# Layer 2's opening: one pipeline over both samples, and a first block whose spectra are formed four rows at a time

## The chip, the cores and the metric

The kernel runs on one core of one Trainium2 chip. The metric is device time in microseconds (us) of that core for one execution of the whole program; several executions are timed and their median is the time of the kernel. A separate profiled execution gives the page and the trace.

## What is computed

Two images of 128 channels by 64 by 64 points, held in the core's memory as X, pass four layers; each adds its output to X after a group normalisation. Layers 0 and 3 are attention over all 4096 points, layer 1 is a set of convolutions. Layer 2, the one concerned here, multiplies quaternion-valued images in the Fourier domain:

```python
xs = jnp.stack([x[:, :q], x[:, q:2 * q], x[:, 2 * q:3 * q], x[:, 3 * q:]])
Xs = jnp.fft.rfft2(xs, s=(GRID_H, GRID_W), axes=(-2, -1))
Ws = jnp.stack([kr_w + 1j * ki_w, kr_x + 1j * ki_x, kr_y + 1j * ki_y, kr_z + 1j * ki_z])
C = jnp.einsum('piohw,qbihw->pqbohw', Ws, Xs)
Pw = C[0, 0] - C[1, 1] - C[2, 2] - C[3, 3]
Px = C[0, 1] + C[1, 0] + C[2, 3] - C[3, 2]
...
o = jnp.fft.irfft2(P, s=(GRID_H, GRID_W), axes=(-2, -1))
```

Every frequency (64 by 33 of them) has its own 128 by 128 real-valued mixing of the channels, so the weights are far larger than the images.

## The kernel before

Layer 2 is the function `_layer2`. All its compute instructions keep the order in which the program text issues them, engine by engine (`_in_order`); an engine that waits holds everything queued behind it. What that order is follows from Python generators: a generator does a piece of work at each step, and `alongside(main, side, steps)` issues `steps` pieces of the side work evenly between the pieces of the main work, and the rest after it.

**Transforms over h** (lines 849 to 895 of the kernel before). For each sample b in turn, the 64 image columns are cut into eight groups of eight. `normalized` (ScalarE, line 860) scales and shifts a group into a tile g; `columns` (TensorE, line 870, and VectorE, line 876) transposes it four times into PSUM and copies it out as gt; `transformed` (TensorE, line 883, and ScalarE, line 884) multiplies by a constant matrix in four matmuls and copies the result into y. A skewed loop issues, in iteration i, `normalized(i)`, `columns(i - 1)` and `transformed(i - 2)`. The loop runs to its end for sample 0 before it begins for sample 1. The statistics of sample 1 (mean and inverse deviation, tile st) are worked out by VectorE, TensorE and GpSimd between the groups of sample 0; from them comes the small tile shift (line 852), which `normalized` reads.

**Blocks of frequencies** (line 897 on). The 32 rows of spectra in y are taken in eight blocks of four. Each block serves two products: one with the rows themselves ("direct", weights of four frequency rows), one with their mirror images. For a row, `transposed` (TensorE line 912, ScalarE line 918) brings y's row into yt, its inner `transformed` (TensorE, line 925) does the transform over w into the PSUM bank pe, and `placed` writes 12 signed copies of it into the tile e (ScalarE, line 948, for the even rows of a pair; VectorE, line 950, for the odd ones). `rows_in` does these for a pair of rows; `copies` does the last of them alone.

`products` (TensorE, line 1008) is 17 steps, one for each pair of frequencies j; a step is four matmuls, one for each row s of the block, each of which writes its own group of 32 output partitions. Each matmul shows as two records in the trace. After j = 3, 7, 11 and 15, and after the last, VectorE transposes the PSUM bank in blocks into z (line 1017), and two VectorE operations form pz (line 1025). The four banks of PSUM are called z0, z4, z8 and z12, two more are tagged bank, two pe.

In the first block the direct rows of both pairs go in ahead of anything else, pair by pair; the mirrored rows are then formed again, transposes and transforms included, beside the first product. The weights of a product (2112 KB twice, line 823) come by DMA from the SP queue into one of two buffers; the load for a product is issued when the product before the last has released its buffer.

Of the kernel before, what the change touches and what calls it, by code (L numbers as in the profile page):

```python
# [10 lines left out]
F32 = mybir.dt.float32  # L11
# [7 lines left out]
CH = 512  # L19
# [783 lines left out]
def _layer2(ctx, tc, X, weights, cst, src, here=None, there=None, beside=None):  # L803
# [26 lines left out]
    with tc.tile_pool(name="l2_a", reuse_waits="tile", bufs=3) as ap, tc.tile_pool(  # L830
        name="l2_aps", reuse_waits="tile", bufs=4, space=PSUM
    ) as aps:
        def stats(b, st):
            return _stats_steps(
                nc,
                ap,
                lambda: aps.tile([128, CH], F32, tag="pt", name="ps_stat"),
                X[:, b, :],
                cst,
                mhalf,  # L840
                st,
            )

        st = here
        if st is None:
            st = ap.tile([128, 2], F32, tag="st", name="st")
            for _ in stats(0, st):
                pass
        for b in range(B):
            xw = X[:, b, :].rearrange("p (h w) -> p w h", w=W)  # L850
            shift = ap.tile([128, 1], F32, tag="shift", name="shift")
            nc.vector.scalar_tensor_tensor(shift, st[:, 0:1], -1.0, st[:, 1:2], ALU.mult, ALU.mult)
            scale = st[:, 1:2]
            if b + 1 < B:
                st = ap.tile([128, 2], F32, tag="st", name="st")
                steps = stats(b + 1, st)

            def normalized(i):
                g = ap.tile([128, 8, H], F32, name="g")
                nc.scalar.activation(  # L860
                    g, xw[:, 8 * i : 8 * i + 8, :], AF.Identity, bias=shift, scale=scale
                )
                for _ in range(2):
                    next(steps, None)
                return g

            def columns(i, g):
                pt = aps.tile([128, CH], F32, tag="pt", name="ps_pt")
                for n in range(4):
                    nc.tensor.transpose(  # L870
                        pt[:, n * 128 : (n + 1) * 128],
                        g[:, 2 * n : 2 * n + 2, :].rearrange("p w h -> p (w h)"),
                        ident,
                    )
                gt = ap.tile([128, CH], F32, name="gt")
                nc.vector.tensor_copy(gt, pt)
                return gt

            def transformed(i, gt):
                py = aps.tile([128, CH], F32, tag="py", name="ps_py")  # L880
                for n in range(4):
                    cols = slice(n * 128, (n + 1) * 128)
                    nc.tensor.matmul(py[:, cols], gt[:, cols], k["fwd_h"], start=True, stop=True)
                nc.scalar.copy(
                    y[:, b, 8 * i : 8 * i + 8, :, :].rearrange("p w c f -> p (w c f)"), py
                )

            gs, gts = {}, {}
            for i in range(W // 8 + 2):
                if i < W // 8:  # L890
                    gs[i] = normalized(i)
                if 1 <= i <= W // 8:
                    gts[i - 1] = columns(i - 1, gs.pop(i - 1))
                if i >= 2:
                    transformed(i - 2, gts.pop(i - 2))

    two = ctx.enter_context(tc.tile_pool(name="l2_two", reuse_waits="tile", bufs=2))
    with tc.tile_pool(name="l2_e", reuse_waits="tile", bufs=4) as ep, tc.tile_pool(
# [21 lines left out]

        def transformed(m, yt):

            pe = bank("pe")
            for b in range(B):
# [64 lines left out]

        def products(ws, e, pz):  # L990

            z = two.tile([128, PAIRS, 2, 4, 16], F32, name="z", bufs=1)
            zf = z.rearrange("p j n a x -> p (j n a x)")
            for j in range(PAIRS):
                last = j == PAIRS - 1
                if j % 4 == 0:
                    ph = bank() if last else pzp.tile([128, CH], F32, tag=f"z{j}", name="ps_z")  # L1000
                for s in range(4):
                    fw = s * FW + 2 * j
# [11 lines left out]
                    )  # L1014
                if j % 4 == 3 or last:
                    lo, n = j // 4 * CH, (j % 4 + 1) * 128
                    nc.vector.transpose(zf[:, lo : lo + n], ph[:, :n])
# [56 lines left out]

        def alongside(main, side, steps):

            done = 0
            for n, _ in enumerate(main):
                while done < steps * (n + 1) / PAIRS:
                    next(side, None)  # L1080
                    done += 1
            for _ in side:
                pass
# [4 lines left out]
        es = [None, None]  # L1088
        first = spectra(0)
        for i in (0, 2):  # L1090
            for _ in rows_in(0, first[i : i + 2], (0,), es):
                pass
        before, later = None, []
        for kb in range(BLOCKS2):
# [10 lines left out]
            else:  # L1105
                later = side
                side, n = [rows_in(0, first[i : i + 2], (1,), e) for i in (0, 2)], 10
            alongside(products(rows_of_weights(kb, False), e[0], pzs[0]), chain(*side), n)
            side, n = [turned(pzs[0], direct)], 4
# [1488 lines left out]
```

## Time and profile before

| what | us |
|---|---|
| median of 3 timed executions | 4012.31 (4012.15 to 4015.99) |
| profiled execution, its own time | 4012.48 |
| its span in the profile | 4010.7 |
| PE / DVE / ACT busy in the span | 3857.8 / 3197.1 / 3247.0 |
| layer 2, first normalisation to last y of the transforms over h | 1795.55 to 1829.78 |
| first block's first product, first and last record | 1837.01 to 1854.39 |
| first block's second product, first record | 1858.84 |

Times within the program are counted from the start of the span. A row of the trace gives the start, the duration, the engine (PE is TensorE, PEld its weight loads, DVE VectorE, ACT ScalarE, POOL GpSimd, SP the queue that issues DMAs), the source line, the operation, what it writes and reads, shapes, and how many records are merged; in brackets stands how long the engine had been idle before it and what released it.

### The profile page before, as it was taken

The numbers are of one execution on the slowest core, as the hardware profiler recorded it, in microseconds if no ns is written. First come the engines' busy times: TensorE is split into PE (matmuls) and PEld (weight loads), VectorE is DVE, ScalarE is ACT, GpSimd is POOL, SyncE is SP. The second block draws the span as 40 slices with busy tenths as digits, with TensorE's granted clock in tenths as the row PEclk, the third lists the DMA queues.
The fourth block names the chain that finished last, engine by engine and source line by source line (L and its number), as shares of the span: only waits on it lengthen the run. The fifth ranks groups of instructions, "written<-read, shape, count | busy, mean of one in ns | idle before, by whom it ended". The sixth has DMA issues, their size and how long they took to land.

```text
span 4010.7 us, 82168 instructions
## 1 busy us (share of the span) xinstructions
PE 3857.8 (96%) x35214; PEld 1318.5 (33%) x35214; DVE 3197.1 (80%) x3572; ACT 3247.0 (81%) x3955; POOL 86.2 (2%) x145
## 2 busy tenths in 40 slices
PE   7999999989999998997998999999999999999998
PEld 4511222353111124445664332232223222322222
DVE  6599999858999998995758777777777777776666
ACT  4499999736899983226645999999999999999998
POOL 1000000000000001000000000000000000000000
PEclk9999999999999999998999999999999999999999
DMA  1199960000000000004654100110002000110000
GB/s 51 24 201 189 187 98 2 1 2 2 2 2 2 2 1 13 6 38 176 268 215 149 33 31 26 53 46 30 27 25 74 30 27 25 43 48 6 6 6 4
DMA packets 193128, 217.59 MB, mean 54 GB/s; under 512 B 30441, under 2 KB 154345, under 8 KB 188658
## 3 DMA queue, kind: packets, MB, share of 16 engines
q1 hardware_dynamic: 192754, 212.25, 20.4%
q8 instruction: 278, 4.55, 0.5%
q14 instruction: 96, 0.79, 0.1%
HBM read 178.64 MB, written 98.57 MB: 69 GB/s over the span
## 4 chain that ended last, share of the span: by engine, by line
PE 81%; DVE 7%; issue 4%; ACT 3%; POOL 0%; DMA 0%; SPq 0%; POOLq 0%; ACTq 0%; DVEq 0%
PE ps_acc L2313 25%; PE ps_s L2290 19%; PE ps L1858 11%; PE ps L1866 11%; PE ps_bank L710 2%; PE ps_z L1008 2%; DVE sums L1889 2%; PE ps L1619 2%; DVE e L950 1%; PE ps_t L640 1%; PE ps_bank L590 1%; PE ps_bank L1062 1%; PE ps_bank L681 1%; PE ps_acc L2171 1%; PE ps_acc L2217 1%
## 5 line engine op out<-in xcount | busy, mean ns | idle before, releaser
L2304 ACT ACTIVATE weights<-ps_s 128x1024 f32<-128x1024 f32 x1920 | 1781.4, 1063 | 76.4 <-PE ps_s L2290 76.2
L2313 PE MATMUL ps_acc<-weights,vt 128*32 128x512 f32 x8192 | 1092.9, 605 | 0.0
L1889 DVE TENSOR_TENSOR sums<-sums,weights 128x2048 f32<-128x2048 f32 x384 | 854.2, 2283 | 3.5 <-ACT weights L1941 1.2
L2290 PE MATMUL ps_s<-q,k 64*128 64x512 f32 x4096 | 830.6, 469 | 4.3 <-DMA k<-stack 2.8
L1941 ACT ACTIVATE weights<-ps 128x1536 f32<-128x1536 f32 x512 | 740.6, 1446 | 6.9 <-PE ps L1866 6.9
L2290 PEld LDWEIGHTS ps_s<-q,k 64*128 64x128 f32 x4096 | 348.4, 184 | 936.6 <-ACT weights L2304 809.4
L1866 PE MATMUL ps<-q,k 32*64 32x512 f32 x8192 | 574.0, 612 | 3.6 <-ACT weights L1938 3.0
L1858 PE MATMUL ps<-weights,vt 128*32 128x512 f32 x4096 | 544.6, 604 | 0.0
L2262 DVE SCALAR_TENSOR_TENSOR exp_z<-exp_z,exp_m 128x1024 f32<-128x1024 f32 x384 | 468.9, 1221 | 9.3
L1938 ACT ACTIVATE weights<-ps 128x512 f32<-128x512 f32 x512 | 306.8, 599 | 75.4 <-PE ps L1866 36.5
L2246 DVE TENSOR_SCALAR exp_i<-ps_s 128x1024 int32<-128x1024 f32 x128 | 156.7, 1224 | 216.4 <-PE ps_s L2290 216.2
L2313 PEld LDWEIGHTS ps_acc<-weights,vt 128*32 128x32 f32 x8192 | 161.9, 108 | 309.3 <-issue 308.5
L1866 PEld LDWEIGHTS ps<-q,k 32*64 32x64 f32 x8192 | 120.0, 129 | 432.1 <-ACT weights L1938 381.6
L1858 PEld LDWEIGHTS ps<-weights,vt 128*32 128x32 f32 x4096 | 84.3, 108 | 390.9 <-issue 378.5
L662 DVE SCALAR_TENSOR_TENSOR X<-g,w,X 128x2048 f32<-128x2048 f32 x84 | 197.4, 2351 | 2.6
L2266 DVE SCALAR_TENSOR_TENSOR weights<-exp_z,exp_i 128x1024 f32<-128x1024 f32 x128 | 156.8, 1225 | 15.9 <-ACT weights L2304 0.5
L1889 DVE TENSOR_TENSOR sums<-weights 128x2048 f32<-128x2048 f32 x64 | 145.7, 2288 | 28.7 <-ACT weights L1941 27.9
L1619 PE MATMUL ps<-pad,diag 32*32 32x512 f32 x4032 | 151.8, 614 | 8.7 <-DVE qk L1630 4.1
L2262 DVE SCALAR_TENSOR_TENSOR exp_z<-exp_m 128x1024 f32<-128x1024 f32 x128 | 155.9, 1218 | 0.0
L1008 PE MATMUL ps_z<-w_ri,e 128*32 128x128 f32 x2048 | 137.5, 409 | 14.6 <-DVE e L950 12.4
L1619 PEld LDWEIGHTS ps<-pad,diag 32*32 32x32 f32 x4032 | 86.2, 104 | 69.2 <-issue 21.1
L950 DVE TENSOR_SCALAR e<-ps_pe 32x136 f32<-32x136 f32 (+1 forms) x352 | 104.4, 297 | 5.0
(314 smaller groups left out, 2953.5 us busy)
## 6 DMA issues: line engine op xcount, KB each, us to landing
w_ri<-w_r SPq DMA_DIRECT2D x16, 2112.0 KB, 7.9
w_ri<-w_i SPq DMA_DIRECT2D x16, 2112.0 KB, 13.7
stack<-qs SPq DMA_DIRECT2D x64, 256.0 KB, 2.1
q<-stack SPq DMA_DIRECT2D x128, 128.0 KB, 2.5
k<-stack SPq DMA_DIRECT2D x128, 128.0 KB, 2.5
stack<-ks SPq DMA_DIRECT2D x32, 256.0 KB, 2.1
w_r<-in_L_conv_kr_w SPq DMA_DIRECT2D x15, 528.0 KB, 12.3
w_r<-in_L_conv_kr_x SPq DMA_DIRECT2D x15, 528.0 KB, 12.5
```

The costliest lines, as they stand in the source:

```text
L662: nc.vector.scalar_tensor_tensor(xi, g[:, i : i + H // 2, j : j + W], w8[:, s : s + 1], xi, ALU.mult, ALU.add)
L1008: nc.tensor.matmul(out.rearrange("p (n f o) -> p n f o", n=2, f=2), e[:, s, 2 * j : 2 * j + 2, :].rearrange("p f x -> p (f x)"), w.rearran ...
L1619: nc.tensor.matmul(ps[r // 2][to, r % 2, :].rearrange("p (h w) -> p h w", w=W), diag[rows, grp, t, :], pad[rows, y0 : y0 + ROWS, t % 3 : t ...
L1858: nc.tensor.matmul(out[rows, :], lhs(rows), w[:, j, :], start=first, stop=stop)
L1866: nc.tensor.matmul(bank[64 * h : 64 * h + 64, :], k1[rows, kt * 128 + 64 * h : kt * 128 + 64 * h + 64], q1[rows, qb * CH : (qb + 1) * CH], ...
L1889: nc.vector.tensor_add(parts[p].rearrange("p j c -> p (j c)"), t.rearrange("p j c -> p (j c)"), w.rearrange("p j c -> p (j c)"),)
L1938: nc.scalar.activation(held[n][:, 0, :], single, AF.Exp)
L1941: nc.scalar.activation(held[n][:, 1:, :], three, AF.Exp)
L2262: nc.vector.scalar_tensor_tensor(z, x, n, m, ALU.add, ALU.mult)
L2290: nc.tensor.matmul(ps[j // 2][:, j % 2, :], g.k[kt // 4][rows, j // 2, keys], g.q[qb][rows, j // 2, :], start=True, stop=True,)
L2304: nc.scalar.activation(w[0], ps[p], AF.Exp)
L2313: nc.tensor.matmul(g.ac[32 * j : 32 * j + 32, :], g.vt[:, kt, j // 2, i : i + 2, :].rearrange("p a d -> p (a d)"), w[:, i, :], start=(at = ...
```

## The change

The loop over samples around the transforms over h becomes one loop over 16 groups, n = 0 to 15, with the same skew of two; the sample is n // 8. The statistics of sample 1 are finished, and its shift formed, ahead of group 8. The copies into y of groups 7, 9, 11, 13 and 15 are issued on VectorE instead of ScalarE.

In the first block all four rows are transposed first and then transformed, rows 3 and 4 into the product banks z8 and z12, since there are only two pe banks. Their direct copies follow without a gap. The mirrored copies of rows 1 and 2 are read from the same pe banks; only rows 3 and 4 are formed again for their mirror. The first block's direct product runs by pairs of rows: rows 1 and 2 for the first 16 frequency pairs, then rows 3 and 4 for the same 16, then the last frequency pair with all four rows, 33 steps in all. Eight pieces of side work are spread over these steps.

```diff
@@ -846,53 +846,65 @@
             st = ap.tile([128, 2], F32, tag="st", name="st")
             for _ in stats(0, st):
                 pass
-        for b in range(B):
-            xw = X[:, b, :].rearrange("p (h w) -> p w h", w=W)
+        def shifted(st):
             shift = ap.tile([128, 1], F32, tag="shift", name="shift")
             nc.vector.scalar_tensor_tensor(shift, st[:, 0:1], -1.0, st[:, 1:2], ALU.mult, ALU.mult)
-            scale = st[:, 1:2]
-            if b + 1 < B:
-                st = ap.tile([128, 2], F32, tag="st", name="st")
-                steps = stats(b + 1, st)
-
-            def normalized(i):
-                g = ap.tile([128, 8, H], F32, name="g")
-                nc.scalar.activation(
-                    g, xw[:, 8 * i : 8 * i + 8, :], AF.Identity, bias=shift, scale=scale
+            return shift
+
+        scales = [st]
+        shifts = [shifted(st)]
+        if B > 1:
+            scales.append(ap.tile([128, 2], F32, tag="st", name="st"))
+            steps = stats(1, scales[1])
+
+        def normalized(n):
+            b, i = divmod(n, W // 8)
+            if i == 0 and b > 0:
+                for _ in steps:
+                    pass
+                shifts.append(shifted(scales[b]))
+            xw = X[:, b, :].rearrange("p (h w) -> p w h", w=W)
+            g = ap.tile([128, 8, H], F32, name="g")
+            nc.scalar.activation(
+                g,
+                xw[:, 8 * i : 8 * i + 8, :],
+                AF.Identity,
+                bias=shifts[b],
+                scale=scales[b][:, 1:2],
+            )
+            for _ in range(2):
+                next(steps, None)
+            return g
+
+        def columns(n, g):
+            pt = aps.tile([128, CH], F32, tag="pt", name="ps_pt")
+            for k4 in range(4):
+                nc.tensor.transpose(
+                    pt[:, k4 * 128 : (k4 + 1) * 128],
+                    g[:, 2 * k4 : 2 * k4 + 2, :].rearrange("p w h -> p (w h)"),
+                    ident,
                 )
-                for _ in range(2):
-                    next(steps, None)
-                return g
-
-            def columns(i, g):
-                pt = aps.tile([128, CH], F32, tag="pt", name="ps_pt")
-                for n in range(4):
-                    nc.tensor.transpose(
-                        pt[:, n * 128 : (n + 1) * 128],
-                        g[:, 2 * n : 2 * n + 2, :].rearrange("p w h -> p (w h)"),
-                        ident,
-                    )
-                gt = ap.tile([128, CH], F32, name="gt")
-                nc.vector.tensor_copy(gt, pt)
-                return gt
-
-            def transformed(i, gt):
-                py = aps.tile([128, CH], F32, tag="py", name="ps_py")
-                for n in range(4):
-                    cols = slice(n * 128, (n + 1) * 128)
-                    nc.tensor.matmul(py[:, cols], gt[:, cols], k["fwd_h"], start=True, stop=True)
-                nc.scalar.copy(
-                    y[:, b, 8 * i : 8 * i + 8, :, :].rearrange("p w c f -> p (w c f)"), py
-                )
-
-            gs, gts = {}, {}
-            for i in range(W // 8 + 2):
-                if i < W // 8:
-                    gs[i] = normalized(i)
-                if 1 <= i <= W // 8:
-                    gts[i - 1] = columns(i - 1, gs.pop(i - 1))
-                if i >= 2:
-                    transformed(i - 2, gts.pop(i - 2))
+            gt = ap.tile([128, CH], F32, name="gt")
+            nc.vector.tensor_copy(gt, pt)
+            return gt
+
+        def transformed(n, gt):
+            b, i = divmod(n, W // 8)
+            py = aps.tile([128, CH], F32, tag="py", name="ps_py")
+            for k4 in range(4):
+                cols = slice(k4 * 128, (k4 + 1) * 128)
+                nc.tensor.matmul(py[:, cols], gt[:, cols], k["fwd_h"], start=True, stop=True)
+            copy = nc.vector.tensor_copy if n > 5 and n % 2 else nc.scalar.copy
+            copy(y[:, b, 8 * i : 8 * i + 8, :, :].rearrange("p w c f -> p (w c f)"), py)
+
+        gs, gts, every = {}, {}, B * (W // 8)
+        for n in range(every + 2):
+            if n < every:
+                gs[n] = normalized(n)
+            if 1 <= n <= every:
+                gts[n - 1] = columns(n - 1, gs.pop(n - 1))
+            if n >= 2:
+                transformed(n - 2, gts.pop(n - 2))
 
     two = ctx.enter_context(tc.tile_pool(name="l2_two", reuse_waits="tile", bufs=2))
     with tc.tile_pool(name="l2_e", reuse_waits="tile", bufs=4) as ep, tc.tile_pool(
@@ -918,9 +930,9 @@
             nc.scalar.copy(yt.rearrange("p b i -> p (b i)"), pt[:, : B * 128])
             return yt
 
-        def transformed(m, yt):
-
-            pe = bank("pe")
+        def transformed(m, yt, pe=None):
+
+            pe = bank("pe") if pe is None else pe
             for b in range(B):
                 nc.tensor.matmul(
                     pe[:, b * 8 * PAIRS : (b + 1) * 8 * PAIRS],
@@ -987,18 +999,22 @@
                     )
                 )
 
-        def products(ws, e, pz):
-
-
-
+        def products(ws, e, pz, by_rows=False):
 
             z = two.tile([128, PAIRS, 2, 4, 16], F32, name="z", bufs=1)
             zf = z.rearrange("p j n a x -> p (j n a x)")
-            for j in range(PAIRS):
+            whole = [(j, range(4)) for j in range(PAIRS)]
+            if by_rows:
+                whole = [(j, s) for s in ((0, 1), (2, 3)) for j in range(PAIRS - 1)] + whole[-1:]
+            phs = {}
+            for j, rows in whole:
                 last = j == PAIRS - 1
-                if j % 4 == 0:
-                    ph = bank() if last else pzp.tile([128, CH], F32, tag=f"z{j}", name="ps_z")
-                for s in range(4):
+                if j % 4 == 0 and rows[0] == 0:
+                    phs[j // 4] = (
+                        bank() if last else pzp.tile([128, CH], F32, tag=f"z{j}", name="ps_z")
+                    )
+                ph = phs[j // 4]
+                for s in rows:
                     fw = s * FW + 2 * j
                     if last:
                         w = ws[:, :, :, fw : fw + 1].to_broadcast([128, 2, 32, 2])
@@ -1012,7 +1028,7 @@
                         start=True,
                         stop=True,
                     )
-                if j % 4 == 3 or last:
+                if (j % 4 == 3 or last) and rows[-1] == 3:
                     lo, n = j // 4 * CH, (j % 4 + 1) * 128
                     nc.vector.transpose(zf[:, lo : lo + n], ph[:, :n])
                 yield
@@ -1072,11 +1088,11 @@
             for g in gens:
                 yield from g
 
-        def alongside(main, side, steps):
+        def alongside(main, side, steps, over=PAIRS):
 
             done = 0
             for n, _ in enumerate(main):
-                while done < steps * (n + 1) / PAIRS:
+                while done < steps * (n + 1) / over:
                     next(side, None)
                     done += 1
             for _ in side:
@@ -1087,8 +1103,13 @@
         ]
         es = [None, None]
         first = spectra(0)
+        yts = [transposed(m) for m in first]
+        places = [None, None] + [
+            pzp.tile([128, CH], F32, tag=f"z{n}", name="ps_z") for n in (8, 12)
+        ]
+        gots = [transformed(m, yt, pe) for m, yt, pe in zip(first, yts, places)]
         for i in (0, 2):
-            for _ in rows_in(0, first[i : i + 2], (0,), es):
+            for _ in copies(0, first[i : i + 2], gots[i : i + 2], (0,), es):
                 pass
         before, later = None, []
         for kb in range(BLOCKS2):
@@ -1104,8 +1125,13 @@
                 n += 6
             else:
                 later = side
-                side, n = [rows_in(0, first[i : i + 2], (1,), e) for i in (0, 2)], 10
-            alongside(products(rows_of_weights(kb, False), e[0], pzs[0]), chain(*side), n)
+                side, n = [copies(0, first[:2], gots[:2], (1,), e), rows_in(0, first[2:], (1,), e)], 8
+            alongside(
+                products(rows_of_weights(kb, False), e[0], pzs[0], kb == 0),
+                chain(*side),
+                n,
+                PAIRS if kb else 2 * PAIRS - 1,
+            )
             side, n = [turned(pzs[0], direct)], 4
             if nxt:
                 side = later + [rows_in(kb + 1, nxt[2:], (1, 0), es)] + side
```

The engines' instruction lists of the changed program differ from those before only in these places: in the order of the transforms over h from group 6 on, and in the first block up to its second product; from there on they are the same, instruction by instruction. Four transposes, four matmuls of the transform over w and two copies into yt fall away.

## The prediction

> **What bounds the kernel now.** I read the page first, for the whole, and then the trace of layer 2's opening alone, because the diff touches nothing else.
>
> ```profile
> span 4010.7 us, 82168 instructions
> PE 81%; DVE 7%; issue 4%; ACT 3%; POOL 0%; DMA 0%; SPq 0%; POOLq 0%; ACTq 0%; DVEq 0%
> ```
>
> TensorE carries 81% of the chain that ended last, nearly all of it in the attention layers, which stay as they are. So the prize is not a share of 4010.7 us; it is what can be cut from the stretch between the first normalisation of layer 2 (1795.55) and the moment from which both programs issue the same instructions in the same order. That moment is the start of the first block's second product, on the mirrored rows: 1858.84. The stretch is 63.3 us. The busy time of its four stages (columns: us, then PE, PEld, DVE, ACT, POOL busy, clock, DMA):
>
> ```profile
> 1795.50:1812.70 17.20, 14.30 (x100) 12.94 (x100) 11.07 (x23) 13.84 (x17) 0.55 (x1) 0.90 1.00 409
> 1812.70:1829.80 17.10, 13.89 (x97) 12.62 (x97) 5.54 (x8) 13.87 (x17) 0.00 (x0) 0.90 0.23 96
> 1829.80:1841.00 11.20, 5.15 (x30) 3.61 (x31) 7.23 (x24) 8.15 (x28) 0.00 (x0) 0.78 0.01 1
> 1841.00:1858.80 17.80, 13.39 (x154) 8.74 (x154) 11.21 (x31) 8.34 (x28) 0.00 (x0) 0.79 0.19 65
> ```
>
> No engine is full in any of them: these are latency-bound stages, so I followed the order of ScalarE, VectorE and TensorE in time. ScalarE at the change of sample:
>
> ```profile
> 1807.75 0.59 ACT L884 COPY y<-ps_py 128x512 f32<-128x512 f32 x1
> 1808.23 1.28 ACT L860 ACTIVATE g<-X,shift,st 128x512 f32<-128x512 f32 x1
> 1809.48 0.59 ACT L884 COPY y<-ps_py 128x512 f32<-128x512 f32 x1
> 1811.16 0.59 ACT L884 COPY y<-ps_py 128x512 f32<-128x512 f32 x1 [1.09 <-PE ps_py L883]
> 1812.20 0.59 ACT L884 COPY y<-ps_py 128x512 f32<-128x512 f32 x1 [0.46 <-PE ps_py L883]
> 1812.69 2.40 ACT L860 ACTIVATE g<-X,shift,st 128x512 f32<-128x512 f32 x2
> ```
>
> Three copies in a row, two of them waiting: the pipeline drains before sample 1 starts. VectorE in the first block:
>
> ```profile
> 1831.90 0.36 DVE L950 TENSOR_SCALAR e<-ps_pe,signs 128x136 f32<-128x136 f32 x1 [3.96 <-PE ps_pe L925]
> 1837.12 0.36 DVE L950 TENSOR_SCALAR e<-ps_pe,signs 128x136 f32<-128x136 f32 x1 [1.45 <-PE ps_pe L925]
> 1846.45 0.72 DVE L1017 STREAM_TRANSPOSE z<-ps_z 128x512 f32<-128x512 f32 x1 [5.57 <-PE ps_z L1008]
> 1853.98 0.72 DVE L1017 STREAM_TRANSPOSE z<-ps_z 128x512 f32<-128x512 f32 x1 [0.64 <-PE ps_z L1008]
> 1857.56 1.23 DVE L950 TENSOR_SCALAR e<-ps_pe 32x136 f32<-32x136 f32 x4
> ```
>
> VectorE stands 1.45 + 5.57 + 0.64 us here, and its last copies of e (the last line) release the second product. TensorE's products, by how many row groups (32 output partitions each) run side by side:
>
> ```profile
> 1837.01 0.65 PE L1008 MATMUL ps_z<-w_ri,e 128*32 128x128 f32 x4
> 1839.82 0.64 PE L1008 MATMUL ps_z<-w_ri,e 128*32 128x128 f32 x2 [2.16 <-ACT e L948]
> 1842.55 0.67 PE L1008 MATMUL ps_z<-w_ri,e 128*32 128x128 f32 x8
> 1858.84 0.66 PE L1008 MATMUL ps_z<-w_ri,e 128*32 128x128 f32 x8 [4.45 <-DVE e L950]
> 1878.82 0.64 PE L1008 MATMUL ps_z<-w_ri,e 128*32 128x128 f32 x6
> 1914.58 0.62 PE L1008 MATMUL ps_z<-w_ri,e 128*32 128x128 f32 x2 [0.88 <-DVE e L950]
> ```
>
> One matmul shows as two records. One group (x2), two (x4), three (x6) and four (x8) all take 0.62 to 0.67 us: groups beside each other are free, and fewer groups save nothing. This decides the forecast.
>
> **What the Trainium skill says.** "TensorE: Matmul & The Clock Gate", section "Measured speedup vs the span model", prices a pack of column tiles at one matmul's duration plus about 4 ns per further tile; the lines above agree (0.64 for one group, 0.67 for four). The same page, "Architectural detail: the array is 16× 32×32, not 1× 128×128", has ScalarE and VectorE as strict FIFO, so a waiting transpose holds the copies behind it; the trace agrees (e copies of 1847.09 stand behind the transpose of 1846.45). Its section "What's actually happening" has the array at half clock after an idle window of about 3.4 us; the trace agrees: four transposes of y take 1.12 us at 1841.51 and 0.71 at 1849.57. "TensorEngine Tiling (Array Packing)", "PSUM Bottleneck", advises both engines for emptying PSUM, which the change does for y; the trace of before has only ScalarE there.
>
> **Part 1: one pipeline over both samples.** Nothing is removed; from the seventh group of columns every odd y copy goes to VectorE (0.69 us, from the gt row of the same shape, against 0.59). Old: g7 starts 1808.23, the copy of y5 1809.48; then the drain, and g8 at 1812.69. New: g8 follows y5 after 0.48 (as 1807.75 to 1808.23), at 1809.96. Its shift now stands behind the seventh gt (end 1809.28) plus 0.15, 1809.43: in time, and the statistics' last step has been done since 1805.34 (1804.79 plus 0.55 on POOL).
>
> Does the rest run faster with ScalarE relieved? Old steady pace: about 1.70 us per group (1806.56, 1808.23; 1821.81, 1823.57, 1825.22). New, per pair: y copy 0.48, g 1.28, 0.05 to the transposes, 0.49 until the py matmuls, 1.06 for these, 0.04 to the next even y copy: 3.40 us. That is 1.70 per group again: the loop through TensorE's queue binds, not ScalarE (which would need 0.48 + 2 × 1.19 = 2.86). So this gives no pace, only the drain. Following it: y6 1811.16, y8 1814.56, y10 1817.96, y12 1821.36, g15 1821.84; the old tail from g15 to the last y is 1829.78 - 1825.22 = 4.56, so y ends at 1826.4. **Gain 3.4 us.** The moved copies ride in VectorE's idle time (5.54 busy of 17.10); without that cover they would cost 5 × 0.69.
>
> **Part 2: four rows of spectra at once, products by pairs.** Times from y's end (old 1829.78 = 0). Old: e of rows 1 and 2 from 1.66 (ScalarE) and 2.12 (VectorE), the second pair from 6.43 and 7.34, done at 11.1; first product's end about 24.6; second product's start 29.06.
>
> New. Four yt copies (0.33 each) instead of two, so e starts about 0.5 later: 2.17 and 2.65. No gap between pairs: ScalarE 2 × 3.55, to 9.3; VectorE 2 × 3.77, to 10.2. The first pair's mirrored copies follow at once, without new transforms (4 transposes, 4 matmuls and 2 yt copies fall away): to 12.9 and 14.0.
>
> TensorE can start rows 0 and 1 at 6.5. But a step (two passes, 0.46: at 1845.26, 32 records, four steps, take 2.05 us; less one record's 0.41, plus the 0.23 between passes, over four, is 0.46 to 0.47) costs the same with two groups as with four. The 17 four-group steps of 7.8 us become 16 + 16 + 1 = 33 steps, 15.2 us. In order: 16 steps, 6.5 to 13.9 (bank z8 free at 9.3, z12 at 10.2, before steps 9 and 13 need them); one step, 14.3; four transposes, 14.9; four steps, 16.7; the last two rows' transforms 1.12, 17.9; then twelve steps.
>
> VectorE's queue from 14.0: first z transpose when step j=3 is done, 16.5; the second stands behind steps j=5 to 7, which stand behind the transforms: 19.5. The mirrored copies of the fourth row are queued behind both. From 19.5 it hardly waits: 0.72, four copies 1.25, z 0.72, four copies 1.23, z 0.72, bank 0.32, the two pz operations 1.15, four copies 1.23, gaps 0.2: 27.0. So the second product starts at about 27.0 instead of 29.06. **Gain 2.1 us** (bounds 1.2 to 3: step 0.48 to 0.43).
>
> **Behind it** all shifts together. Weights: the third load is issued at the first product's end, 23.4, that is 3.6 us ahead of the second product instead of 4.4; old it was issued at 1854.44 and landed by about 1868 for a first use at 1878.82, and no product ever waits for a DMA, so 0.8 us costs nothing. SP's and POOL's instructions keep their order.
>
> Sum: 3.4 + 2.1 = 5.5 us. The profiled execution took 4012.48, so 4007.0; from the median shown, 4012.31, that is **4006.8**.
>
> **Rivals.** (a) Pairs are cheap: if two groups need half a step (0.23), rows 0 and 1 wait only for the banks, z4 is ready at about 15.7 and the second product starts at 23.1: part 2 gives 6.0, in all 9.4, 4002.9. For it: the one two-group line (x4) shows two passes of one matmul, not a run of different ones. Against: one, three and four groups agree, at both clocks (0.62 and 0.64 at full, 0.64 and 0.67 at half).
> (b) Little but the drain is won: TensorE stays at half clock through the thinner products, and the mirrored rows' transposes and transforms cost 1.12 + 2.18 (as at 1841.51 and 1843.15) instead of 0.6 + 1.12. That is 1.6 us before z4, so part 2 keeps 0.5: 3.9 in all, 4008.4; uncounted gaps could take another 2.
> (c) ScalarE's relief does raise the pace, to 2.86 per pair: 0.54 × 4 = 2.2 more, 4004.6. Against: the 3.40 loop.
> (d) Slower: half clock doubles a pair's step s. Once s is over about 0.49, TensorE sets every z transpose, and by the order above the second product starts at 12.1 + 32 s. At 0.92 that is 41.5, a loss of 12.4; less 3.4, 4021.3. Slower than before from s = 0.63 on. Against: passes at half clock kept the same 0.64 to 0.67.
>
> **How the numbers follow.** Forecast 0.62 (own range 4005 to 4008.5), (a) 0.18, (b) 0.11, (c) 0.05, (d) 0.04. A measurement of this kernel tells about 0.2%, 8.0 us, from no change; the forecast lies inside it, (a) outside. Faster 0.24 ((a), and (c) with some of the forecast's far end), same 0.71, slower 0.05. Range 4001.5 to 4010.8: (a) to most of (b).
>
> **What would show it.** Right: no run of three y copies; g8 about 0.5 after y5; y ends near 1826.4; pace still 3.4 per pair with ScalarE waiting for ps_py; pair products of 32 matmuls spread over about 7.4 us; VectorE idle before the first two z transposes; second product near 1853.4. A pair run of about 4 us would mean (a); pairs of g closer than 3.4, (c). Wrong altogether if the interval from second product to the end changes by more than 1 us.

## The result, and the profile after

The changed kernel takes 4005.05 us (median of 12 executions, 3999.97 to 4010.81) against 4013.56 us for the kernel before (12 executions, 4008.67 to 4018.16). The ratio is 0.9978, with a 95% interval of 0.9971 to 0.9985. Of 4012 us that is 8.8 us less, between 6.0 and 11.6; the two medians themselves differ by 8.5. The forecast was 5.5 us less. Both kernels scatter by about 10 us from one execution to the next, more than the three first timings of the kernel before had shown (4012.15 to 4015.99).

Inside the stretch that the change touches, the profile comes out almost where the prediction put it. The windows of the profile after, for the transforms over h and for the first block up to its second product (columns: us, then PE, PEld, DVE, ACT, POOL busy, clock, DMA):

```profile
1795.60:1826.60 31.00, 26.15 (x197) 23.85 (x197) 20.06 (x36) 24.97 (x27) 0.55 (x1) 0.94 0.68 280
1826.60:1853.20 26.60, 20.63 (x174) 13.28 (x175) 18.57 (x55) 15.74 (x54) 0.00 (x0) 0.94 0.10 27
```

The two stages took 34.2 and 29.1 us before; they take 30.9 and 26.6 now. The second product starts 57.5 us after the first normalisation instead of 63.3: **5.8 us** of the 8.8 are here, 3.3 by the pipeline and 2.5 by the first block.

ScalarE at the change of sample, in the timeline of the kernel after:

```profile
1809.59 0.59 ACT L898 COPY y<-ps_py 128x512 f32<-128x512 f32 x1
1810.07 1.28 ACT L868 ACTIVATE g<-X,shift,st 128x512 f32<-128x512 f32 x1
1811.25 0.59 ACT L898 COPY y<-ps_py 128x512 f32<-128x512 f32 x1
1811.73 2.46 ACT L868 ACTIVATE g<-X,shift,st 128x512 f32<-128x512 f32 x2
1814.66 0.59 ACT L898 COPY y<-ps_py 128x512 f32<-128x512 f32 x1 [0.46 <-PE ps_py L896]
1815.14 2.45 ACT L868 ACTIVATE g<-X,shift,st 128x512 f32<-128x512 f32 x2
1818.05 0.59 ACT L898 COPY y<-ps_py 128x512 f32<-128x512 f32 x1 [0.46 <-PE ps_py L896]
```

The run of three copies is gone: group 8 starts 0.48 after the copy before it. From 1814.66 to 1818.05 are 3.39 us for two groups, and ScalarE, relieved of every second copy, stands 0.46 us per pair waiting for TensorE. So the relief bought no pace.

VectorE in the first block:

```profile
1829.26 0.36 DVE L962 TENSOR_SCALAR e<-ps_pe,signs 128x136 f32<-128x136 f32 x1 [2.69 <-PE ps_pe L937]
1833.06 0.36 DVE L962 TENSOR_SCALAR e<-ps_z,signs 128x136 f32<-128x136 f32 x1
1836.86 0.36 DVE L962 TENSOR_SCALAR e<-ps_pe,signs 128x136 f32<-128x136 f32 x1
1842.73 0.72 DVE L1033 STREAM_TRANSPOSE z<-ps_z 128x512 f32<-128x512 f32 x1 [2.10 <-PE ps_z L1024]
1845.78 0.72 DVE L1033 STREAM_TRANSPOSE z<-ps_z 128x512 f32<-128x512 f32 x1 [2.33 <-PE ps_z L1024]
1851.86 1.22 DVE L962 TENSOR_SCALAR e<-ps_pe 32x136 f32<-32x136 f32 x4
```

The gap of 1.45 us between the pairs has gone, and the wait of 5.57 has become two, of 2.10 and 2.33, before the first two transposes of z. TensorE shows why they did not go altogether:

```profile
1832.40 8.17 PE L1024 MATMUL ps_z<-w_ri,e 128*32 128x128 f32 x68 [2.25 <-ACT e L960]
1841.14 2.00 PE L1024 MATMUL ps_z<-w_ri,e 128*32 128x128 f32 x16
1843.07 1.19 PE L937 MATMUL ps_pe<-consts,yt 128*128 128x136 f32 x8
1844.19 4.54 PE L1024 MATMUL ps_z<-w_ri,e 128*32 128x128 f32 x38
1853.18 0.67 PE L1024 MATMUL ps_z<-w_ri,e 128*32 128x128 f32 x8 [3.31 <-issue]
```

The first 17 steps by pairs (68 records) take 8.17 us. Less one record's 0.41, plus the 0.23 between passes, that is 0.47 per step. A step of four rows cost the same before, where four of them (32 records) took 2.05 us:

```profile
1845.26 2.05 PE L1008 MATMUL ps_z<-w_ri,e 128*32 128x128 f32 x32
```

TensorE's granted clock, the share of full speed that the profile records for it, is either 1 or 0.5 in these traces. It stood at 0.5 over the first part of the pairs and at 1 over the rest (columns as above):

```profile
1832.80:1836.10 3.30, 3.25 (x29) 2.10 (x30) 3.15 (x11) 3.16 (x12) 0.00 (x0) 0.50 0.00 0
1836.30:1840.40 4.10, 4.10 (x40) 2.22 (x36) 3.91 (x14) 3.15 (x12) 0.00 (x0) 1.00 0.00 0
```

In both parts the passes follow each other every 0.23 us, so half clock did not lengthen a pair's step.

The span shrank by 9.3 us (4010.7 to 4001.4), and 3.65 us of that lie after the second product, where both programs issue the same instructions. Half of the experiments ask what these are.

### The profile page after: what moved, and what is told of

It reads as the page before. It is cut to its first block, busy times and chain, and to the rows that moved or that the text cites. A ratio compares the mean times of both kernels' runs of the same rounds, so it can differ in the third digit from the quotient of the medians.

```text
span 4001.4 us, 82144 instructions
## 1 busy us (share of the span) xinstructions
PE 3853.4 (96%) x35202; PEld 1313.9 (33%) x35202; DVE 3200.6 (80%) x3577; ACT 3243.5 (81%) x3948; POOL 86.2 (2%) x145
## 4 chain that ended last, share of the span: by engine, by line
PE 78%; DVE 10%; issue 4%; ACT 2%; POOL 0%; SPq 0%; DMA 0%; ACTq 0%; POOLq 0%; DVEq 0%
PE ps_acc L2339 25%; PE ps_s L2316 19%; PE ps L1884 11%; PE ps L1892 11%; DVE X L662 3%; PE ps_z L1024 2%; PE ps_bank L710 2%; DVE sums L1915 2%; PE ps L1645 2%; DVE e L962 1%; PE ps_bank L681 1%; PE ps_bank L1078 1%; PE ps_acc L2197 1%; PE ps_acc L2243 1%; PE ps_pe L937 1%
```

## The experiments

Theory A is that each part gives what its stage shows, and that what follows is the same stream of instructions, whose length scatters. Its rivals are that the pairs carry the gain (P) and that an earlier start shortens what follows in a regular way (R). Two more came later: that the length of what follows depends on where its start falls in the grid of 3.41 us on which the granted clock changes (W), and, against it, that it differs by chance or by what the first block does (S).

Kernels that were run together ran on one chip, beside the kernel before. All columns but the last are from the profile; times are in us. "Stretch" is the time from the first g to the second product, in two parts. "Rest" is the time from the second product to layer 2's last stage (the first zt), and "to the end" the time from the second product to the end of the program; both hold the same instructions in every kernel. "Phase" is the time from the last line of the clock's grid to the start of the rest, so that 3.4 and 0 are the same place. "Clock" is TensorE's mean granted clock in the rest.

| kernel | to last y | to second product | stretch | phase | rest | clock | to the end | ratio to before, 95% interval |
|---|---|---|---|---|---|---|---|---|
| before | 34.2 | 29.1 | 63.3 | 2.3 | 242.4 | 0.91 | 2151.9 | 1 |
| before, again | 34.3 | 29.3 | 63.6 | 2.8 | 238.7 | 0.94 | 2148.9 | 0.9999 (0.9991 to 1.0007) |
| changed | 30.9 | 26.6 | 57.5 | 3.4 | 238.5 | 0.94 | 2148.2 | 0.9978 (0.9971 to 0.9985) |
| changed, again | 30.9 | 26.6 | 57.5 | 0.1 | 238.3 | 0.94 | 2147.9 | 0.9972 (0.9961 to 0.9982) |
| changed, third | 30.9 | 26.6 | 57.5 | 0.1 | 239.9 | 0.92 | 2151.9 | 0.9977 (0.9968 to 0.9986) |
| pipeline alone | 30.9 | 29.4 | 60.4 | 3.0 | 241.9 | 0.91 | 2151.3 | 0.9987 (0.9979 to 0.9995) |
| first block alone | 34.2 | 26.6 | 60.8 | 3.4 | 238.4 | 0.94 | 2147.7 | 0.9985 (0.9978 to 0.9991) |
| whole rows | 30.8 | 24.7 | 55.4 | 0.6 | 244.2 | 0.90 | 2156.9 | 0.9978 (0.9970 to 0.9986) |
| copies on ScalarE | 30.9 | 26.5 | 57.4 | 3.2 | 243.2 | 0.91 | 2158.1 | 0.9984 (0.9974 to 0.9993) |
| products first | 45.3 | 26.6 | 72.0 | 0.1 | 238.3 | 0.94 | 2148.2 | 1.0017 (1.0011 to 1.0023) |
| skew of three | 30.5 | 26.6 | 57.1 | 2.3 | 245.8 | 0.90 | 2158.8 | 0.9986 (0.9978 to 0.9994) |
| whole rows, skew of three | 29.0 | 24.7 | 53.7 | 3.2 | 241.7 | 0.91 | 2150.9 | 0.9983 (0.9975 to 0.9990) |
| before, 1.2 us added | 34.2 | 30.2 | 64.4 | 0.1 | 238.3 | 0.94 | 2148.2 | 1.0002 (0.9994 to 1.0010) |
| changed, 1.8 us added | 30.8 | 28.4 | 59.2 | 0.9 | 240.3 | 0.92 | 2150.5 | 0.9999 (0.9990 to 1.0007) |

### The two parts alone

The pipeline alone: the first hunk of the change, up to the line that opens the pool `l2_two`; the first block stays as before.

> The one pipeline over both samples alone; the first block as before. Theory A (each part gives what its stage shows, what follows is the same stream): the last y near 1826.5, the first block keeps its 29.1 us, the second product starts near 1855.6; 3.3 us less than before. Rival R (an earlier start also shortens the rest of layer 2 in a regular way): the second product at the same 1855.6, but 5 us or more less in all. Rival P (the pairs and the four rows carry the gain, the pipeline nothing): within 1 us of before.

Measured: stretch 60.4 (30.9 + 29.4), time 4006.81 against 4012.64. The last y comes 3.3 us sooner, as theory A has it; the first block is 0.4 longer than in the first profile of the kernel before and 0.2 longer than in its second, so that 2.9 us are left of the stretch.

The first block alone: all hunks after that line, with the loop over samples as before.

> The first block's change alone; the transforms over h as before, sample by sample. Theory A: last y at 1829.8, second product 26.6 us later, 1856.4; 2.4 us less than before. Rival R: 4 us or more less. Rival P: 5.5 us less, second product near 1853.5.

Measured: stretch 60.8 (34.2 + 26.6), time 4006.64. In the profile the parts give 2.9 and 2.5 us, together the changed kernel's 5.8 within half a microsecond, so they hardly interact. Rival P falls, since the pipeline alone is not within 1 us of before. In time the parts give 5.2 (2.0 to 8.4) and 6.0 us (3.6 to 8.8), each more than its stage and each what rival R had forecast (5 or more, 4 or more). The second interval excludes 2.5, so the time holds something besides the stage.

### Pairs against whole rows

```diff
-                products(rows_of_weights(kb, False), e[0], pzs[0], kb == 0),
+                products(rows_of_weights(kb, False), e[0], pzs[0]),
...
-                PAIRS if kb else 2 * PAIRS - 1,
+                PAIRS,
```

> The changed kernel with the first block's direct product by whole rows again: 17 steps of four matmuls, none before all four rows of e are there. Theory A (a pair's step costs as much as a whole one): the product cannot start before 10.3 us after the last y, but has 17 steps in place of 33; by the order of its queues the second product starts 24.4 us after the last y, 2.2 us earlier than with pairs; about 8 us less than before. Rival P (the early start by pairs is what gains): the second product about 3.7 us later than with pairs, 30 us after the last y, and only 2 us less than before.

Measured: 24.7 us from the last y to the second product, against 26.6 with pairs and 29.1 before. This is a verdict on the pairs: they cost 1.9 us rather than gaining any. Without them, forming four rows at once gives 4.4 us in the first block. TensorE's timeline with whole rows:

```profile
1836.38 4.33 PE L1024 MATMUL ps_z<-w_ri,e 128*32 128x128 f32 x66 [0.27 <-DVE e L962]
1850.77 0.66 PE L1024 MATMUL ps_z<-w_ri,e 128*32 128x128 f32 x8 [4.37 <-DVE e L962]
```

and VectorE's:

```profile
1838.90 0.72 DVE L1033 STREAM_TRANSPOSE z<-ps_z 128x512 f32<-128x512 f32 x1
1844.15 0.72 DVE L1033 STREAM_TRANSPOSE z<-ps_z 128x512 f32<-128x512 f32 x1 [2.54 <-PE ps_z L1024]
```

Apart from a few matmuls of the first step, the product waits for the last row, and then 33 matmuls go in 4.33 us where the pairs took 8.17 for 34. The first transpose of z finds its bank full. In time this kernel and the changed one can't be told apart (0.9978 both): the rest took 244.2 us in this profile.

### The pace of the pipeline

All copies into y on ScalarE:

```diff
-            copy = nc.vector.tensor_copy if n > 5 and n % 2 else nc.scalar.copy
+            copy = nc.scalar.copy
```

> The changed kernel with all copies into y on ScalarE, as before the change. The prediction's loop through TensorE's queue (3.40 us per two groups): the last y within 0.3 us of the changed kernel's, 30.9 us after the first g, and the same time in all. Rival (the copies on VectorE quicken the pipeline): the last y 2 us later.

Measured: last y after 30.9 us, as with the copies on VectorE. So moving them to a second engine gains nothing in this stage, and the advice to empty PSUM by both engines, which the prediction named, does not pay here. ScalarE's timeline in this kernel, one group every 1.70 us or so without a wait:

```profile
1813.51 0.59 ACT L898 COPY y<-ps_py 128x512 f32<-128x512 f32 x1
1813.99 1.28 ACT L868 ACTIVATE g<-X,shift,st 128x512 f32<-128x512 f32 x1
1815.19 0.59 ACT L898 COPY y<-ps_py 128x512 f32<-128x512 f32 x1
1815.67 1.28 ACT L868 ACTIVATE g<-X,shift,st 128x512 f32<-128x512 f32 x1
```

Here ScalarE looks like the bound, and with half the copies moved away it waits instead: there are two bounds of nearly equal length, of which the change lifts one.

To lift the other I first exchanged the two calls of the loop:

```diff
-            if 1 <= n <= every:
-                gts[n - 1] = columns(n - 1, gs.pop(n - 1))
             if n >= 2:
                 transformed(n - 2, gts.pop(n - 2))
+            if 1 <= n <= every:
+                gts[n - 1] = columns(n - 1, gs.pop(n - 1))
```

> The changed kernel with the two calls of the loop exchanged, so that TensorE multiplies group n-2 before it transposes group n-1. The loop through TensorE's queue is cut: ScalarE's 0.48 + 2 x 1.19 or TensorE's own work sets the pace, 2.9 us for two groups in place of 3.40, and the last y comes about 28.5 us after the first g instead of 30.9. If the loop was not what bound it: 30.9 still. In all, theory W: the second product then starts at phase 0.9 of the grid and the rest takes 242 to 244 us, so that the time is 2 to 3 us above the changed kernel's. Rival S: 2.4 us below it.

Measured: last y after 45.3 us, 14.4 later than in the changed kernel, and a time 0.17% longer than that of the kernel before. My expectation was wrong, and TensorE's timeline shows how:

```profile
1817.87 1.16 PE L896 MATMUL ps_py<-consts,gt 128*128 128x128 f32 x8 [0.78 <-DVE gt L888]
1818.86 0.60 PE L882 MATMUL ps_pt<-consts,g 128*128 128x128 f32 x4
1820.25 1.16 PE L896 MATMUL ps_py<-consts,gt 128*128 128x128 f32 x8 [0.78 <-DVE gt L888]
```

Each multiplication now waits for VectorE's copy of the very group transposed just before it, and the next transposes stand behind that multiplication: a round trip of 2.38 us per group, in place of 1.70. With one group more in flight that copy lies further back:

```diff
-        for n in range(every + 2):
+        for n in range(every + 3):
...
+            if n >= 3:
+                transformed(n - 3, gts.pop(n - 3))
             if 1 <= n <= every:
                 gts[n - 1] = columns(n - 1, gs.pop(n - 1))
-            if n >= 2:
-                transformed(n - 2, gts.pop(n - 2))
```

> The changed kernel with a skew of three groups in place of two, and TensorE's products of group n-3 issued before the transposes of group n-1. The exchange alone put each product behind the copy of the group just transposed (a round trip of 2.4 us per group); with one group more in flight that copy has long been done. If a round trip through TensorE's queue sets the pace, the steady pace falls from 3.40 us per two groups to 2.9 (ScalarE's 0.48 + 2 x 1.19) and the last y comes 28 to 29 us after the first g instead of 30.9; if ScalarE or something else sets it, 30.9 stays. In all: 2.4 us less than the changed kernel where what follows is alike; but what follows has scattered by 6 us with the half-clock windows, so 0 to 8 us less than before the change, with 240 to 244 us from the second product to layer 2's last stage expected at this phase.

> Whole rows in the first block's direct product and the skew of three together. The two gains add: last y 28.5 us after the first g, second product 24.7 us after that, 53.2 in all against 63.3 before and 57.5 with the change. 10 us less than before if what follows is as long as before (242 us to layer 2's last stage), 6 to 14 with its scatter. If the two share a bound: 55 or more.

ScalarE in the second of these, with whole rows:

```profile
1810.44 0.57 ACT L898 COPY y<-ps_py 128x512 f32<-128x512 f32 x1
1810.91 2.45 ACT L868 ACTIVATE g<-X,shift,st 128x512 f32<-128x512 f32 x2
1813.26 0.57 ACT L898 COPY y<-ps_py 128x512 f32<-128x512 f32 x1
1813.73 2.46 ACT L868 ACTIVATE g<-X,shift,st 128x512 f32<-128x512 f32 x2
1816.10 0.57 ACT L898 COPY y<-ps_py 128x512 f32<-128x512 f32 x1
```

2.82 to 2.84 us for two groups and no wait: the loop through TensorE's queue was what bound the changed pipeline at 3.40, and with it gone ScalarE's own work does. Not all of it reaches the last y (29.0 and 30.5 instead of the 28.5 expected): the head of the pipeline got slower, where in the skew-of-three kernel a copy of y waits 2.69 us for TensorE, which itself waits 2.25 for the statistics of sample 1. The stretch of both edits together is the shortest of all, 53.7, 9.6 us under the kernel before; its time, 4005.93 against 4012.72, is no better than the changed kernel's. I have no version that is shown to beat the change.

### What lies after the stretch

> The changed kernel once more, unaltered. Theory A: the second product again at 1853.2, and the rest of the program, which is the same stream of instructions in all these kernels, of a length that scatters by a few us from one execution to the next; 5.7 us less than before. Rival R: the rest again shorter than with the kernel before by some 3 us; 8.8 us less.

Measured: 4001.65 against 4012.64, and 238.3 us of rest. By itself this spoke for rival R. But the kernels with one part each had rests of 241.9 and 238.4, and whole rows, with the earliest start of the four, 244.2. The granted clock in the rest goes with its length. In all 14 profiles taken together, the time at half clock in the rest is 30.6 or 30.7 us in the six with the shortest rests (238.3 to 238.7) and 38.5 to 50.2 us in the others. One window each of before, before again, changed, changed a third time, and skew of three (columns as above):

```profile
1858.80:2101.20 242.40, 219.22 (x2598) 148.22 (x2599) 163.44 (x448) 138.06 (x414) 0.00 (x0) 0.91 0.62 247
```

```profile
1857.70:2096.50 238.80, 215.93 (x2599) 144.71 (x2599) 163.53 (x448) 137.79 (x415) 0.00 (x0) 0.94 0.63 250
```

```profile
1853.20:2091.70 238.50, 215.07 (x2598) 144.12 (x2599) 163.46 (x448) 138.00 (x414) 0.00 (x0) 0.94 0.64 253
```

```profile
1852.30:2092.10 239.80, 216.67 (x2598) 146.15 (x2599) 163.38 (x448) 138.15 (x414) 0.00 (x0) 0.92 0.63 251
```

```profile
1855.50:2101.40 245.90, 222.49 (x2598) 151.47 (x2599) 163.38 (x448) 138.09 (x415) 0.00 (x0) 0.90 0.62 245
```

Every engine has as many records to within one; VectorE and ScalarE are busy for the same time within 0.4 us, TensorE from 215.1 to 222.5; and the lower the clock in these five, the longer the rest. The clock changes on a grid: in the kernel before at 1856.52, 1863.35, 1870.17, 1873.59 and 1880.41, which are 6.83, 6.82, 3.42 and 6.82 us apart, whole multiples of 3.41, and so on through layer 2 in all 14 traces. To move the start of the rest within this grid I put an idle VectorE operation ahead of the last copies of e (950 columns in the kernel before, 1560 in the changed one; the argument `pause` is given for the first direct product alone):

```diff
+            if pause:
+                nc.vector.tensor_tensor(zf[:, :pause], zf[:, :pause], zf[:, :pause], ALU.max)
             yield
```

> The kernel before with one idle VectorE operation more (an in-place maximum of 950 columns of z with itself, about 1.05 us) ahead of the last copies that release the first block's second product; nothing else differs. Theory W (what follows the second product is the same stream, but its length depends on where its start falls in the 3.41 us grid on which the granted clock changes: 238.4 us from there to layer 2's last stage at phase 0, 242 to 244 elsewhere): the start moves from phase 2.3 to about 3.4, that is 0, the rest shortens by about 3.9, and the kernel with more work is about 2.8 us faster than before. Rival S (the rest differs by chance, or by what the first block does): 1.1 us slower than before.

> The changed kernel with the same kind of operation, 1560 columns, about 1.7 us, at the same place. Theory W: the second product starts at phase 1.7 of the grid instead of 0, the rest takes 242 to 244 us instead of 238.4, and the kernel is 5 to 7 us slower than the changed one, 4 to 6 us faster than before at most by g's own start. Rival S: 1.7 us slower than the changed one.

In the profile of the first, theory W came true: the start moved to phase 0.1 and the rest fell to 238.3, so that the profiled execution was faster than that of the kernel before with more work in it (span 4008.0 against 4010.7). In time it did not: the interval, 2.4 us faster to 4.0 slower, leaves out W's 2.8 us faster and holds S's 1.1 slower. In the second the start came at phase 0.9 instead of the 1.7 intended, and the rest at 240.3, not 242 or more. Its time rose to the kernel before's, by the ratios some 8 us over the changed kernel's, which is nearer to W's 5 to 7 than to S's 1.7; none of its 13 executions took under 4008.5 us, where the fastest of the changed kernel took 4000. So one test speaks against W in time and the other for it. Two more profiles ask what each kernel does by itself:

> The changed kernel a third time, beside the two others. 57.5 us from the first g to the second product again. If what follows is a matter of the half-clock windows of each execution, 238 to 244 us after it in the profile, and a time 5 to 9 us below the kernel before; a fixed further gain of 3 us would show as 238.4 once more and 8.8 us or more below.

> The kernel before, unaltered, as a control of the measurement and for a second profile of it. 63.3 us from the first g to the second product, as in its first profile. If what follows is a matter of the half-clock windows of each execution: the rest may come out anywhere from 2148 to 2158 us (2151.9 in its first profile). If the kernel before has a rest of its own, 3 us longer than the changed one's: 2151.9 once more, within 0.5. In time: the ratio to itself within 0.1% of 1.

The changed kernel's third profile starts its rest at the same phase as its second (0.14 us in both) and takes 239.9 instead of 238.3, and from layer 2's last stage to layer 3's first exponentials 45.3 instead of 42.5; in all, from the second product to the end, 2151.9 against 2147.9. The kernel before's second profile has 238.7 where its first had 242.4, and 2148.9 to the end where it had 2151.9. From the second product to the end each kernel thus shows both lengths, 2152 and some 2148 to 2149, so rival R falls as a rule: the change does not shorten what follows it in a fixed way.

The phases of all 14 profiles say more than the two tests. Six start within 0.14 us of a line of the grid: five have rests of 238.3 to 238.5, and one has 239.9. Of the eight others, one has 238.7 and seven have 240.3 to 245.8. All three profiles of the changed kernel are among the six, neither of the kernel before. I grouped them after the fact, and the phase does not settle the length by itself: starts at 2.31 and 2.32 were followed by 245.8 and 242.4. Nor is the rest the only part that scatters: ahead of the first g, too, all programs are the same, and it came between 1792.8 and 1798.8 us.

**What stays open.** In time the changed kernel was 8.8, 11.2 and 9.2 us faster in its three groups of runs (the ratios times 4012 us), with intervals that begin at 6.0, 7.2 and 5.6; its stretch gives 5.8. With the copies on ScalarE the stretch is the same, and the time 6.4 us less (2.8 to 10.4). Not even the fastest executions follow the stretch: on the chip that ran them together, those of pipeline alone, first block alone, changed and whole rows were 3.0, 3.2, 6.8 and 6.5 us below the fastest of the kernel before, with stretches 2.9, 2.5, 5.8 and 7.8 shorter. That the changed kernel should meet a shorter rest more often than the kernel before is what these numbers suggest.

The timed executions, too, are longer where their mean clock is lower. Of the 30 of the changed kernel, the 14 with a mean of 0.987 over the whole program took 4001.7 us on average, the 7 with 0.985 or less 4008.5; of 45 of the kernel before, the 20 with 0.985 took 4011.0, the 12 with 0.983 or less 4017.4. Whether the clock is the cause of the length is not shown by this, since no run held the clock fixed.

## Why the prediction came out as it did

- **The drain, gain 3.4.** This was right: g8 starts 0.48 us after the copy before it (0.48 said), the last y ends at 1826.57 (1826.4 said), and 3.3 us are gained.
- **No gain in pace, loop of 3.40.** This was right, and it is shown from both sides: two groups take 3.39 us, all copies on ScalarE give the same last y, and with the loop cut two groups take 2.83. Rival (c), a pace of 2.86 from the relief alone, is refuted.
- **A pair's step costs 0.46.** This was right: it costs 0.47, and whole rows, 17 steps in place of 33, start the second product 1.9 us sooner. Rivals (a), cheap pairs, and (d), pairs at double cost, are refuted. "TensorE: Matmul & The Clock Gate", section "Measured speedup vs the span model" of the Trainium skill, prices each further column tile of one pack at about 4 ns. It gives no price for packs that follow each other; there the trace shows 0.47 us with two tiles and 0.46 to 0.47 with four, so further tiles cost next to nothing here as well. What the prediction did not ask is how the same block would do without pairs.
- **First block, gain 2.1.** This was right within the bounds given: 2.5. The second product starts 26.6 us after the last y (27.0 said), and VectorE waits before the first two transposes of z as said, at 1842.73 and 1845.78, that is 16.2 and 19.2 us after the last y (16.5 and 19.5 said).
- **Rivals (b) and (d), half clock through the pairs.** Half clock did come, for 3.4 of the 8.2 us of pairs, but not the loss that either rival drew from it: a pass took 0.23 us at both clocks, and the mirrored rows' transposes and transforms came after it at full clock (0.71 us for four transposes at 1840.50). The mean clock of the stage was 0.94, against 0.78 before.
- **"Behind it all shifts together."** This is the term that was mis-sized. It is true of the instructions and not of their time: the rest of layer 2 takes 238.3 to 245.8 us for the same stream. The 5.5 us became 8.8 by the ratio; 0.3 of the difference is in the stretch and 3.0 outside it. The prediction's own sign of being wrong altogether, a change of more than 1 us between the second product and the end, did come: 2151.9 became 2148.2. But two profiles of the kernel before differ there by 3.0 us and three of the changed kernel by up to 4.0, so the sign could not tell a wrong prediction from scatter. I had read the clock's windows as a cost inside the first block only, when the windows before told of them in the next blocks too (0.83, 0.83, 0.66 and 0.87 in the four stretches of 10 us from 1860 on).
- **The range.** The forecast's ratio, 0.9986, lies just outside the measured interval. The measured ratio times 4012.31 is 4003.5, below the forecast's own range of 4005 to 4008.5. The whole range held by luck: it had been drawn out to rival (a)'s 4002.9, for a reason that turned out false.
- **No measurable change, 8.0 us.** This bound was too coarse. Twelve executions of each kernel give an interval of 6.0 to 11.6 us less, which excludes no change although each kernel scatters by about 10.

## What to carry to other kernels

Where a product is made of column tiles side by side, as here, splitting it by tiles to start it early doubled its steps without making them shorter. Count steps, not matmuls, and compare with waiting for all tiles. In a pipeline over in-order engines, relieving an engine that looks full helps only if no loop through the other queues is as long: add up one round trip from a copy to the same copy, and if it equals the pace, put another group in flight. And a gain of a few us ahead of long work whose length scatters with the clock is judged in the profile by its own stage: in time the first block alone gave 6.0 us for 2.5, and whole rows no more than the changed kernel for 2.1 us of shorter stretch.

## What I had not expected of the hardware

A stretch of the same 2598 matmul records took 238.3 to 245.8 us, 3% apart, with a granted clock of 0.94 to 0.90, in executions of kernels that differ only ahead of it, and 238.7 and 242.4 in two executions of one program. Two executions that began it at the same phase of the clock's grid, to 0.01 us, still came out 1.6 us apart. Passes of two column tiles came every 0.23 us at half clock as at full clock. And 1.8 us of idle work added to the changed kernel cost it all that it had gained (0.9999 of the kernel before, 0.9990 to 1.0007).
